# Four graph layers in one kernel: small steps at the seam between layer 0 and layer 1 put in another order

## The chip, the cores and the metric

The kernel runs on one core of a Trainium2 chip. The metric is the device time of one execution in microseconds; less is better. A core has five engines with a queue each, which run side by side and wait for one another by semaphores: TensorE (PE in the profile; its weight loads are PEld), VectorE (DVE), ScalarE (ACT), GpSimd (POOL) and SyncE (SP), which here only issues DMAs. ScalarE issues DMAs too. An engine works off its queue in order: an instruction that waits holds everything behind it.

## What is computed

`x` is 2708 x 128 and `adj` 2708 x 2708, f32, about 0.6% of it not zero. Four layers each add a graph network's answer to `x`; the change touches the end of layer 0 and the beginning of layer 1.

```python
# layer 0
h = relu(layernorm(x))
x = x + (adj.T @ h) / adj.sum(axis=0)[:, None]        # 1/deg, 0 where it is infinite
# layer 1
h = relu(layernorm(x))
s = h @ msg_w[:, :D].T                                # sources, by row i
d = h @ msg_w[:, D:].T                                # destinations, by column j
messages   = gelu(s[:, None, :] + d[None, :, :] + msg_b)
aggregated = einsum('ijd,ij->id', messages, adj)
u = gelu(concat([h, aggregated]) @ upd_w.T + upd_b) + h
x = x + layernorm(u) * ln_w + ln_b
# layer 2: GRU cell on relu((adj @ h) @ W_msg.T + b_msg); layer 3: two attention heads, masked by adj
```

## The kernel before

Rows are cut into 22 tiles of 128 (the last has 20 rows), and these into six groups of four (`GROUPS`, the last of two). All order is written out by hand; there is no scheduler that moves instructions.

**Layer 0** goes over sets (c, s): 512 columns `c` by the 512 rows of group `s`. For c = 0 to 4 the loop at L733 takes each set in turn. `load_cut` (L314) brings it in on SP, five sets ahead. `list_cut` (L344) lets DVE find, per row and block of 128 columns, the eight largest values (`val`, L356) and their places (`col`, L358). `work_cut` (L366) has TensorE transpose the set block by block into PSUM (`p_T`, L403, three banks), ScalarE copy each transposed strip to `aT` with its sum (the degrees, L410) and send it to memory as `adjT` (L364), and TensorE multiply the set with `h` (L388). The narrow last columns (c = 5, 148 wide, tiles `z`) are loaded early, and their sets are worked in pieces (`PARTS`) behind sets (4,1) to (4,4).

`work_cut` takes a second argument, a generator of small steps; after each `aT` copy it runs one of them. `next_steps(c, s)` (L516) gives these for c > 0: copy the finished sums of the group before (`lift`), scale and add them to `x` (`spread`, which needs `inv_deg` from `invert` on DVE), then sums and squares over the rows (`sum_rows`, `sum_squares`, the latter ending in a chain of GpSimd steps on `flat`), then the normalized rows of layer 1 (`normal_rows`). A group of layer 1's rows is turned (`turn_rows`), multiplied into destinations (`destinations`, bf16 lead `d`), and the rest split off in two further bf16 parts (`take_lead` L247 on DVE, `split_rest` L253 on ScalarE and L254 on GpSimd).

**Layer 1** works on the listed edges only. For each row tile t one needs:

- `count_some` or `count_rows`: how many entries each row has in each block (`rows_n`), on DVE; `rank` (L551): a matmul that sums these counts over the rows before, giving `ends`; `spread_ends` (L558): a copy of `ends` four times over
- `select_rows` (L601): a 128 x 2816 comparison that makes `sel`, the row of every edge slot; its shifted copy `later` goes by DMA (L620, L621); `finish_rows` (L625) subtracts it
- the values in three bf16 parts in `xb`, of which there are two, by the parity of t: `lead_of` (ScalarE, L568), `less_lead` (DVE, L586, into a tile named `hot`), `pass_rest` (ScalarE L590, GpSimd L591, and `describe_columns`, GpSimd L580 and L581)
- `fetch` (L639): 22 small matmuls `y<-xb,sel` that move values and columns to edge slots; `place` (L652 to L673, DVE) picks `value` and `where` from them
- `pass_on` and `spread_columns`: `where` is transposed, copied (`where_T`, L691), written to memory (`passed`, L693) and read back to all partitions (`spread`, L699); `columns` (L973, DVE) compares it to `cols`
- `put_values` (L956, eight GpSimd steps) and `put_more` (L965, ScalarE): the value of each edge placed on its row.

Then `period(t, opening)` (L1127) runs row tile t's main work in six pieces k: `combine` (L1012 with `sel` and the sources `s`, L1016 with `cols` and the destinations `d`) into `p_m` (two banks), GELU on ScalarE (`g`, L1024), `gather` (L1037), with the preparation of tiles t+1 to t+4 in between. Period 0 differs: its opening steps stand in a table (`opening`, L1231), run at the head of each k, and what periods before it would have prepared is made during layer 0 and in the `run(...)` list ahead of the periods (L1226).

So the last sets of layer 0 carry steps of layer 1: `count_some` and `list_last` in (4,0) to (4,2), `rank(0, 3)` of three tiles in (4,1), `select_rows(0)` after it, `finish_rows(0)` after (4,2), `pass_rest(0)` and `fetch(0)` after (4,3), `place(0)` after (4,4), `last_destinations` within (4,5), and a list of small steps at the end of layer 0 (L813 to L826).

PSUM banks of the pool `ps` are two and go round: `p_r`, the two `y` of tile 0, `p_h`, `p_d`, `p_w` and `p_s` take turns, each waiting until the one before last has been read.

Of the kernel before, what the change touches and what calls it, by code (L numbers as in the profile page):

```python
# [30 lines left out]
P = 128  # L31
# [14 lines left out]
S = 8  # L46
# [14 lines left out]
def listed_layers(ctx: ExitStack, tc: tile.TileContext, x, adj, w, out, flag):  # L61
# [8 lines left out]
    def bank(name):  # L70
        return ps.tile([P, CH], F32, tag="ps", name=name)
# [194 lines left out]
    def sum_squares(g):  # L266
        t, k = GROUPS[g]
        for q in range(t, t + k):
            junk = pool.tile([P, D], F32, name="junk")
            nc.scalar.activation(  # L270
                junk, xs[:, q, :], AF.Square, bias=flat[:, 0, q : q + 1], accum_out=flat[:, 1, q : q + 1]
            )
            if q == t + k - 1:
                shift, ve, rstd, tmp = (flat[:, r, t : t + k] for r in range(4))
                nc.gpsimd.tensor_scalar(ve, ve, 1.0 / D, EPS, ALU.mult, ALU.add)
                nc.gpsimd.tensor_tensor(rstd, ve, minus_half[:, 0:k], ALU.pow)
                nc.gpsimd.tensor_tensor(tmp, rstd, rstd, ALU.mult)
                nc.gpsimd.tensor_tensor(tmp, tmp, ve, ALU.mult)
                nc.gpsimd.tensor_scalar(tmp, tmp, -0.5, 1.5, ALU.mult, ALU.add)
                nc.gpsimd.tensor_tensor(rstd, rstd, tmp, ALU.mult)  # L280
                nc.gpsimd.tensor_tensor(shift, shift, rstd, ALU.mult)
            yield

    def normal_rows(dst, g, rstd=None, shift=None):
        t, k = GROUPS[g]
        for q in range(k):
            r, b = (flat[:, 2, t : t + k], flat[:, 0, t : t + k]) if rstd is None else (rstd, shift)
            scale_rows([dst[:, t + q, 0:D]], [xs[:, t + q, :]], r[:, q : q + 1], b[:, q : q + 1], AF.Relu)
            yield
# [226 lines left out]
    def next_steps(c, s):  # L516

        off = 1 if c < LAST - 1 else 0
        stage = s - 1 - off
        if stage == -1:  # L520
            return lift(c - 1)
        if stage == 0:
            return spread(c - 1)
        if stage == 1:
            return sum_rows(c - 1)
        if stage == 2:
            return sum_squares(c - 1)
        if stage == 3:
            return normal_rows(h, c - 1)
        return last_destinations() if stage == 4 and c == LAST - 1 else ()  # L530

    def last_destinations():
        destinations(LAST - 2)
        yield
        pass_on(0)
        project(0)
        turn_sums(LAST)
        yield

    def list_last(n):  # L540
# [41 lines left out]

    def less_lead(t):
        dst, src = values_of(t)
        rest = state["x", t] = opener.tile([P, NB, S], F32, name="hot")
        nc.vector.tensor_tensor(rest, src, dst[0], ALU.subtract)  # L586

    def pass_rest(t):
# [93 lines left out]
    def pass_on(t):  # L682

        st = state[t]
        if t == 0:
            p = ps.tile([P, 2 * CH], BF16, tag="ps", name="p_w")
        else:
            p = rpool.tile([P, 2 * CH], BF16, tag="r", name="p_w")
        nc.tensor.transpose(p[:, 0:E], st.pop("where"), ident_h)
        turned_w = own_tile(t, [NB, E], BF16, "where_T")  # L690
        nc.scalar.copy(turned_w, p[0:NB, 0:E])  # L691
        st["passed"] = wdram.tile([NB, E], BF16, name="passed")
        nc.sync.dma_start(st["passed"], turned_w)  # L693
# [39 lines left out]
    for i, (c, s) in enumerate(order):  # L733
        g0, gk = GROUPS[s]
        list_cut(c, s, g0)
        if i == 0:
            state["f", 0] = factors(*state.pop(("m", -1)))
            list_cut(c, s, g0 + 1)
            state["m", 1] = moments(tiles_of(xs, *GROUPS[1]), "n4")
            list_cut(c, s, g0 + 2)  # L740
            state["f", 1] = factors(*state.pop(("m", 1)))
            list_cut(c, s, g0 + 3)
        else:
            for n in range(g0 + 1, g0 + gk):
                if c > 0 and s == (2 if c < LAST - 1 else 1) and n == g0 + 1:
                    invert(c - 1)
                list_cut(c, s, n)
            if c == LAST - 1:
                for n in {0: range(FIRST), 1: range(FIRST, 4), 2: range(4, HELD), LAST: range(NT - 2, NT)}.get(s, ()):
                    list_last(n)  # L750
                if s == 0:
                    count_some(0, FIRST)
                if s == 1:
                    count_some(FIRST, 1)
        if i + 1 < len(order):
            mask_near(*order[i + 1])
        if i > BEHIND and i - 1 - BEHIND + RING < len(order):
            load_cut(*order[i - 1 - BEHIND + RING])
        for z in {(LAST - 2, 3): (0,), (LAST - 2, 4): (1,), (LAST - 2, 5): (2,), (LAST - 1, 0): (3,), (LAST - 1, 2): (4,), (LAST - 1, 3): (5,)}.get(
            (c, s), ()  # L760
        ):
            load_cut(LAST, z)
        if (c, s) == (LAST - 1, 2):
            shift_rows(0)
        if c > 0 and s == (2 if c < LAST - 1 else 1):
            turn_sums(c - 1)
        if (c, s) == (LAST - 1, LAST):
            turn_rows(LAST - 2)
        work_cut(c, s, first_steps(s) if c == 0 else next_steps(c, s))
        if c > 1 and s == 3:  # L770
            split_rest(c - 2)
        if (c, s) == (LAST - 1, 3):
            pass_rest(0)
        if c > 1 and s == 0:
            turn_rows(c - 2)
        if c > 1 and s == 1:
            destinations(c - 2)
        if c > 1 and s == 2:
            take_lead(c - 2)
        if c == LAST - 1:  # L780
            if s == 1:
                ranked = rank(0, FIRST, bank("p_r"))
            for z in PARTS.get(s, ()):
                mask_near(LAST, z)
                work_cut(LAST, z)
            if s == 1:
                nc.vector.tensor_copy(*ranked)
                spread_ends(0)
                select_rows(0)
                lead_of(*values_of(0))  # L790
            if s == 2:
                less_lead(0)
                finish_rows(0)
            if s == 3:
                for q in range(2):
                    fetch(0, q)
            if s == LAST - 1:
                place(0)
                lead_of(*values_of(2))
                less_lead(2)  # L800
                for _ in lift(LAST):
                    pass

        if (c, s) == (1, 2):
            nc.sync.dma_start(msg_wT, w["msg_wT"])
        if (c, s) == (2, 3):
            nc.sync.dma_start(msg_b, w["msg_b"].partition_broadcast(P))
            nc.gpsimd.tensor_copy(src_self[:, 0, :], msg_wT[:, 0, :])
            nc.gpsimd.tensor_tensor(src_self[:, 1, :], msg_wT[:, 0, :], msg_wT[:, 1, :], ALU.add)

    write_one()

    pass_rest(2)  # L813
    lead_of(*values_of(1))
    take_lead(LAST - 2, pool.tile([P, 4, D], F32, bufs=1, name="part_x"))
    add(LAST)
    measure(LAST)
    less_lead(1)
    add_bias(0, d_rest.rearrange("p (t c) d -> p t c d", t=2))
    spread_ends(1)  # L820
    split_rest(LAST - 2)
    for _ in lift(LAST - 1):
        pass
    turn_sums(LAST - 1)
    rows(LAST)
    pass_rest(1)  # L826
    ending.close()
    l0.close()

# [31 lines left out]
    with (  # L861
# [265 lines left out]
        def period(t, opening):  # L1127
# [6 lines left out]
            for k in range(GB):  # L1134
# [3 lines left out]
                if k == 0 and c and begun:  # L1138
                    pass_on(t + 1)
                    spread_columns(t + 1)  # L1140
                if k == 1 and a:
                    nc.vector.tensor_copy(*rank(t + 3, 1, rpool.tile([P, CH], F32, tag="r", name="p_r")))
                    spread_ends(t + 3)
                if k == 1 and last:
# [23 lines left out]
                if k == 2:  # L1168
                    if now and t % 2 == 0 and t + 2 < NT:
                        sources(t // 2 + 1)  # L1170
                    if a and begun:
                        select_rows(t + 3)
                        describe_rest(t + 3)
                    if now and t % 2 == 0 and t + 2 < NT:
                        sources_rest(t // 2 + 1)
                    if now and t + 4 < NT - 2:
                        count_rows(t + 4)
                if k == 1 and t == NT - 2:
                    check_lists()
# [43 lines left out]
        def take_pair(g):  # L1223
# [6 lines left out]
        )  # L1230
        opening = {  # L1231
            1: ((turn_rows, 4), (fetch_both, 1), (select_rows, 2), (put_more, 0, 1)),
            2: ((destinations, 4), (put_more, 0, 2), (put_more, 0, 3), (place, 1), (take_lead, 4), (finish_rows, 2)),
            3: ((split_rest, 4), (pass_on, 1), (spread_columns, 1), (put_more, 0, 4), (put_more, 0, 5)),
            4: ((fetch_both, 2), (find_rows, 1), (put_values, 1)),
            5: ((place, 2),),
        }
# [880 lines left out]
```

## Time and profile before

| | us |
|---|---|
| median of 3 runs | 987.94 (986.31 to 989.44) |
| the profiled execution | 986.58 |
| its span on the core | 984.8 |
| TensorE busy, granted clock | 911.1 (93%), 0.968 |
| VectorE busy | 797.0 (81%) |
| ScalarE busy | 531.8 (54%) |
| GpSimd busy | 444.1 (45%) |

The page of the profile gives the busy time of each engine, a picture of the span in 40 slices, and the costliest groups of instructions. The answers on the trace give the same by stretch of time, and timelines: start, busy time, engine, line and operation, and in brackets how long the engine stood idle before it and what released it. A releaser is inferred: where a matmul that had long been done is named, it was another, often a DMA. By the timeline, layer 0's last product on TensorE (L388) ends at 195.87 us, period 0 begins in earnest at 205.76, and period 1 at 230.53. The stretches around these, with the busy time of each engine, the granted clock of TensorE and the DMA engines' share:

| stretch, us | PE | DVE | ACT | POOL | PE clock | DMA |
|---|---|---|---|---|---|---|
| 170 to 175 | 3.81 | 5.00 | 5.00 | 1.20 | 1.00 | 0.70 |
| 175 to 180 | 1.40 | 5.00 | 1.00 | 4.59 | 0.82 | 0.24 |
| 195 to 200 | 2.23 | 4.79 | 2.07 | 2.50 | 0.87 | 0.41 |
| 200 to 205 | 1.93 | 4.61 | 3.51 | 2.27 | 0.50 | 0.59 |
| 215 to 220 | 3.72 | 2.98 | 1.61 | 1.35 | 1.00 | 0.05 |
| 220 to 225 | 0.79 | 4.95 | 4.41 | 4.66 | 0.76 | 0.14 |
| 225 to 230 | 5.00 | 4.05 | 2.48 | 5.00 | 0.56 | 1.01 |

### The profile page before, as it was taken

The numbers are of one execution on the slowest core, as the hardware profiler recorded it, in microseconds if no ns is written. First come the engines' busy times: TensorE is split into PE (matmuls) and PEld (weight loads), VectorE is DVE, ScalarE is ACT, GpSimd is POOL, SyncE is SP. The second block draws the span as 40 slices with busy tenths as digits, with TensorE's granted clock in tenths as the row PEclk, the third lists the DMA queues.
The fourth block names the chain that finished last, engine by engine and source line by source line (L and its number), as shares of the span: only waits on it lengthen the run. The fifth ranks groups of instructions, "written<-read, shape, count | busy, mean of one in ns | idle before, by whom it ended". The sixth has DMA issues, their size and how long they took to land. (4 is left out here: it accounts for less than half of the span.)

```text
span 984.8 us, 21973 instructions
## 1 busy us (share of the span) xinstructions
PE 911.1 (93%) x7948; PEld 742.5 (75%) x7948; DVE 797.0 (81%) x2753; ACT 531.8 (54%) x1561; POOL 444.1 (45%) x524
## 2 busy tenths in 40 slices
PE   6799999768999999899999999999789999999983
PEld 3465556558999999898999444444678999999972
DVE  7999999788988989889674756566689877997793
ACT  5766776656666756676566123433222553655242
POOL 5402221369976787969765634444111300430132
PEclk9999999978999999999999899999899999999996
DMA  9899998325543434323215355564301674456000
GB/s 334 286 354 365 359 368 296 125 94 160 169 129 117 149 115 135 120 81 132 91 62 190 119 190 208 194 237 134 93 6 57 211 245 151 145 186 208 1 17 15
DMA packets 81736, 163.61 MB, mean 166 GB/s; under 512 B 9100, under 2 KB 27056, under 8 KB 81618
## 3 DMA queue, kind: packets, MB, share of 16 engines
q1 hardware_dynamic: 62518, 129.98, 40.8%
q10 hardware_dynamic: 19100, 32.13, 9.0%
q8 instruction: 64, 1.05, 0.5%
q14 instruction: 54, 0.44, 0.1%
HBM read 115.47 MB, written 30.87 MB: 149 GB/s over the span
## 5 line engine op out<-in xcount | busy, mean ns | idle before, releaser
L1327 PE MATMUL att<-hv,wt 128*128 128x129 f32 x1672 | 195.7, 278 | 7.9 <-DVE wt L1297 6.4
L956 POOL TENSOR_SCALAR put<-count,line,value 128x128 f32<-128x128 f32 x176 | 197.6, 1134 | 11.1 <-DVE value L673 10.4
L1327 PEld LDWEIGHTS att<-hv,wt 128*128 128x128 f32 x1672 | 191.9, 194 | 10.9 <-DVE wt L1297 8.9
L1016 PE MATMUL p_m<-d,cols 128*128 128x128 bf16 (+1 forms) x1452 | 162.6, 221 | 9.2 <-DVE cols L973 4.3
L1012 PE MATMUL p_m<-s,sel 128*128 128x128 bf16 x1452 | 162.4, 221 | 5.0 <-ACT g L1024 4.9
L1297 DVE SCALAR_TENSOR_TENSOR wt<-row,lift,mask 128x1024 f32<-128x1024 f32 (+1 forms) x132 | 138.8, 1083 | 22.2 <-PE att L1327 22.2
L121 POOL TENSOR_TENSOR n_r<-n_r,minus_half 128x4 f32<-128x4 f32 (+1 forms) x28 | 38.9, 1389 | 237.7 <-DVE n_r L120 236.0
L1037 PE MATMUL agg<-put,g 128*128 128x128 f32 (+1 forms) x968 | 126.8, 284 | 0.0
L1037 PEld LDWEIGHTS agg<-put,g 128*128 128x128 f32 x968 | 116.2, 196 | 2.4 <-issue 0.2
L388 PE MATMUL sums<-a,h 128*128 128x512 f32 x220 | 113.9, 613 | 1.6 <-ACT h L137 1.6
L1488 PE MATMUL p_agg<-a,hs 128*128 128x512 f32 (+2 forms) x264 | 108.8, 554 | 2.8 <-DMA a<-adjT 2.8
L1012 PEld LDWEIGHTS <-sel 128*128 128x128 bf16 x1452 | 103.9, 99 | 9.0 <-issue 8.3
L1016 PEld LDWEIGHTS <-cols 128*128 128x128 bf16 (+1 forms) x1452 | 101.9, 99 | 10.1 <-DVE cols L973 5.0
L1024 ACT ACTIVATE g<-p_m 128x512 f32<-128x512 f32 x132 | 72.7, 552 | 63.8 <-PE agg L1037 45.0
L403 PEld LDWEIGHTS p_T<-ident,a 128*128 128x128 f32 (+1 forms) x440 | 55.4, 144 | 60.7 <-issue 43.1
L965 ACT ACTIVATE put<-mine,value 128x128 f32<-128x128 bf16 x308 | 100.6, 392 | 0.0
L358 DVE FIND_INDEX8 col<-val,a 128x8 uint16<-128x128 f32 x327 | 91.6, 298 | 0.0
L410 ACT ACTIVATE aT<-p_T 128x512 f32<-128x512 f32 (+2 forms) x132 | 71.1, 541 | 27.5 <-PE p_T L403 26.6
L1488 PEld LDWEIGHTS p_agg<-a,hs 128*128 128x128 f32 (+1 forms) x264 | 47.5, 193 | 50.6 <-issue 46.3
L403 PE MATMUL p_T<-ident,a 128*128 128x128 f32 (+1 forms) x440 | 70.5, 281 | 11.9 <-DMA a<-in_adj 6.2
L1450 ACT ACTIVATE hs<-hs 128x1354 f32<-128x1354 f32 (+1 forms) x44 | 58.5, 1330 | 39.9 <-DMA hs<-in_adj 39.5
L356 DVE MAX8 val<-a 128x8 f32<-128x128 f32 x327 | 79.4, 289 | 0.0
(297 smaller groups left out, 1529.0 us busy)
## 6 DMA issues: line engine op xcount, KB each, us to landing
hs<-in_adj SPq DMA_DIRECT2D x42, 677.0 KB
adjT<-aT ACTq DMA_DIRECT2D x50, 512.0 KB
a<-adjT SPq DMA_DIRECT2D x20, 1280.0 KB
a<-in_adj SPq DMA_DIRECT2D x24, 1024.0 KB
spread<-passed SPq DMA_DIRECT2D x22, 704.0 KB
later<-sel SPq DMA_DIRECT2D x22, 616.0 KB
cols_a<-in_adj SPq DMA_DIRECT2D x11, 320.0 KB
row<-own_d ACTq DMA_DIRECT2D x10, 256.0 KB
```

What stands on the lines that cost most here:

```text
L356: nc.vector.max(val[0:m, n, b, :], v)
L358: nc.vector.max_index(col[0:m, n, b, :], val[0:m, n, b, :], v)
L388: nc.tensor.matmul(accs[c][:, 0:w], h0[0:m, n, :], a[0:m, n - g0, t0 * P - lo : t0 * P - lo + w], start=(n == 0), stop=(n == NT - 1),)
L403: nc.tensor.transpose(p[0:k, i * iw + q * P : i * iw + q * P + m], a[0:m, q, e : e + k], ident[0:m, 0:m])
L956: nc.gpsimd.tensor_scalar(st["put", 0][:, b, :], count, st["line"][:, b : b + 1], st["value"][:, b : b + 1], ALU.is_equal, ALU.mult,)
L965: nc.scalar.activation(st["put", 1][:, b - HP, :], st["mine"][:, b - HP, :], AF.Identity, scale=st["value"][:, b : b + 1])
L1012: nc.tensor.matmul(p[:, b - b0, :], st["sel"][:, b, :], s3[:, q, t % 2, :], start=(q == 0), stop=False)
L1016: nc.tensor.matmul(p[:, b - b0, :], st["cols"][0:kb, b, :], d3[0:kb, b, q, :], start=False, stop=(q == 2))
L1037: nc.tensor.matmul(agg, g[:, b - 4 * k, :], put, start=(b == 0), stop=False)
L1297: nc.vector.scalar_tensor_tensor(wt[:, 0:n], row[:, k, c : c + n], lift[:, j, k : k + 1], mask[:, j, c : c + n], op0=ALU.max, op1=ALU.mult,)
L1327: nc.tensor.matmul(banks[s // 3][:, s % 3, :], wt[:, q * P : (q + 1) * P], hv[:, j, k, :], start=(v < 2 and s // 3 not in touched), stop=( ...
L1488: nc.tensor.matmul(pa[:, 0:n], h[0:k, j, :], a[0:k, j - j0, 0:n], start=(j == 0), stop=(j == NT - 1))
```

## The change

No arithmetic is changed. The steps that move:

- Ranks of four row tiles at once: `list_last(3)` and `count_some(3)` move from set (4,1) to (4,0), `rank` covers tiles 0 to 3, tile 4 is counted in set (4,2), and period 0 loses its rank matmul and its `count_rows(4)`.
- `pass_rest(0)` becomes the first small step within set (4,3); before it came behind the whole set.
- `project(0)` and the leads of tiles 2 and 1 become the first small step within set (4,4).
- `turn_rows(3)` moves between the two z parts behind (4,4), and `destinations(3)` and `pass_on(0)` ahead of set (4,5).
- `less_lead(1)` (now into a tile named `picked`), `spread_ends(1)` and `add_bias(0)` follow `place(0)` and `less_lead(2)`; `pass_rest(2)`, `pass_rest(1)` and `turn_sums(5)` become the first small step within set (4,5).
- In period 0's opening, `split_rest(4)` and `finish_rows(2)` change places: the first goes to the head of k=2, the second to that of k=3.

```diff
         if stage == 2:
-            return sum_squares(c - 1)
+            squares = sum_squares(c - 1)
+            return in_turn(in_order((pass_rest, 0)), squares) if c == LAST - 1 else squares
         if stage == 3:
-            return normal_rows(h, c - 1)
-        return last_destinations() if stage == 4 and c == LAST - 1 else ()
-
-    def last_destinations():
-        destinations(LAST - 2)
-        yield
-        pass_on(0)
-        project(0)
-        turn_sums(LAST)
+            last = c == LAST - 1
+            return in_turn(in_order((project, 0), (lead_of, *values_of(2)), (lead_of, *values_of(1))), normal_rows(h, c - 1)) if last else normal_rows(h, c - 1)
+        if stage == 4 and c == LAST - 1:
+            return in_order((pass_rest, 2), (pass_rest, 1), (turn_sums, LAST))
+        return ()
+
+    def in_order(*steps):
+
+        for step, *numbers in steps:
+            step(*numbers)
         yield
...
     def less_lead(t):
         dst, src = values_of(t)
-        rest = state["x", t] = opener.tile([P, NB, S], F32, name="hot")
+        if t == 1:
+            rest = opener.tile([P, NB, 4, S], F32, name="picked").rearrange("p b q s -> p (b q s)")[:, 0 : NB * S]
+            rest = rest.rearrange("p (b s) -> p b s", s=S)
+        else:
+            rest = opener.tile([P, NB, S], F32, name="hot")
+        state["x", t] = rest
         nc.vector.tensor_tensor(rest, src, dst[0], ALU.subtract)
...
-                for n in {0: range(FIRST), 1: range(FIRST, 4), 2: range(4, HELD), LAST: range(NT - 2, NT)}.get(s, ()):
+                for n in {0: range(FIRST + 1), 2: range(4, HELD), LAST: range(NT - 2, NT)}.get(s, ()):
                     list_last(n)
                 if s == 0:
                     count_some(0, FIRST)
-                if s == 1:
                     count_some(FIRST, 1)
+                if s == 2:
+                    count_some(FIRST + 1, 1)
...
         if (c, s) == (LAST - 1, LAST):
-            turn_rows(LAST - 2)
+            destinations(LAST - 2)
+            pass_on(0)
         work_cut(c, s, first_steps(s) if c == 0 else next_steps(c, s))
         if c > 1 and s == 3:
             split_rest(c - 2)
-        if (c, s) == (LAST - 1, 3):
-            pass_rest(0)
...
-                ranked = rank(0, FIRST, bank("p_r"))
+                ranked = rank(0, FIRST + 1, bank("p_r"))
             for z in PARTS.get(s, ()):
                 mask_near(LAST, z)
                 work_cut(LAST, z)
+                if z == LAST - 1:
+                    turn_rows(LAST - 2)
...
                 place(0)
-                lead_of(*values_of(2))
                 less_lead(2)
+                less_lead(1)
+                spread_ends(1)
+                add_bias(0, d_rest.rearrange("p (t c) d -> p t c d", t=2))
...
-    pass_rest(2)
-    lead_of(*values_of(1))
     take_lead(LAST - 2, pool.tile([P, 4, D], F32, bufs=1, name="part_x"))
     add(LAST)
     measure(LAST)
-    less_lead(1)
-    add_bias(0, d_rest.rearrange("p (t c) d -> p t c d", t=2))
-    spread_ends(1)
     split_rest(LAST - 2)
...
     rows(LAST)
-    pass_rest(1)
...
-                if k == 1 and a:
+                if k == 1 and a and not begun:
+                    spread_ends(t + 3)
+                elif k == 1 and a:
                     nc.vector.tensor_copy(*rank(t + 3, 1, rpool.tile([P, CH], F32, tag="r", name="p_r")))
                     spread_ends(t + 3)
...
-                    if now and t + 4 < NT - 2:
+                    if now and begun and t + 4 < NT - 2:
                         count_rows(t + 4)
...
-            2: ((destinations, 4), (put_more, 0, 2), (put_more, 0, 3), (place, 1), (take_lead, 4), (finish_rows, 2)),
-            3: ((split_rest, 4), (pass_on, 1), (spread_columns, 1), (put_more, 0, 4), (put_more, 0, 5)),
+            2: ((destinations, 4), (put_more, 0, 2), (put_more, 0, 3), (place, 1), (take_lead, 4), (split_rest, 4)),
+            3: ((finish_rows, 2), (pass_on, 1), (spread_columns, 1), (put_more, 0, 4), (put_more, 0, 5)),
```

## The prediction

> **What bounds the kernel now.** I read the page's slices first, to find the stage in which the change lives.
>
> ```profile
> PE   6799999768999999899999999999789999999983
> DVE  7999999788988989889674756566689877997793
> PEclk9999999978999999999999899999899999999996
> ```
>
> A slice is 24.6 us. TensorE is at 9 nearly everywhere; the weak stretch is slices 7 to 9 (172 to 246 us): the end of layer 0 and period 0 of layer 1, where every edit lies. From 230 us to 300 us TensorE is busy without a gap (busy time by stretch), so an earlier start of period 1 is kept. TensorE's own timeline for 172 to 226 us shows the holes:
>
> ```profile
> 178.60 0.86 PE L639 MATMUL y<-xb,sel 128*128 128x37 bf16 x22 [4.76 <-POOL xb L581]
> ...
> 199.06 0.70 PE L150 MATMUL p_h<-ident,hs 128*128 128x128 f32 x2 [1.85 <-ACT hs L137]
> ...
> 205.76 0.50 PE L1016 MATMUL p_m<-d,cols 128*128 128x128 bf16 x3 [3.51 <-DVE cols L973]
> ...
> 218.31 0.72 PE L639 MATMUL y<-xb,sel 128*128 128x37 bf16 x22 [0.54 <-DVE sel L625]
> ...
> 221.86 0.22 PE L1016 MATMUL p_m<-d,cols 128*128 128x128 bf16 x1 [2.60 <-ACT d L253]
> 224.42 0.27 PE L1016 MATMUL p_m<-d,cols 128*128 128x128 bf16 x1 [2.35 <-POOL d L254]
> ```
>
> The bracket is TensorE's idle time and its releaser. The timeline of all engines tells what delayed the first releaser:
>
> ```profile
> 170.24 0.34 DVE L586 TENSOR_TENSOR hot<-val,xb 128x176 f32<-128x176 f32 x1
> 173.72 0.19 POOL L275 TENSOR_SCALAR flat<-flat 128x4 f32<-128x4 f32 x1 [8.85 <-ACT junk L270]
> 174.03 0.37 ACT L590 CAST xb<-hot 128x176 bf16<-128x176 f32 x1
> 176.39 1.15 POOL L254 TENSOR_TENSOR d<-d_r,d 128x512 bf16<-128x512 f32 x1
> 177.50 0.54 POOL L591 TENSOR_TENSOR xb<-hot,xb 128x176 bf16<-128x176 f32 x1
> ```
>
> `hot` is ready at 170.58; ScalarE copies it at 174.03 behind a set of sums, and GpSimd takes it at 177.50 behind the `flat` chain and `d`. In period 0:
>
> ```profile
> 216.62 1.62 DVE L625 TENSOR_TENSOR sel<-sel,later 128x2816 bf16<-128x2816 bf16 x1 [1.46 <-DMA later<-sel]
> 218.88 0.40 ACT L568 CAST s<-sb 128x256 bf16<-128x256 f32 x1 [2.83 <-DVE sb L728]
> 221.20 0.60 ACT L253 CAST d<-d_r 128x512 bf16<-128x512 f32 x1
> 221.88 2.49 POOL L254 TENSOR_TENSOR d<-d_r,d 128x512 bf16<-128x512 f32 x1
> 227.68 1.05 DVE L973 TENSOR_SCALAR cols<-spread,part 128x2816 bf16<-128x2816 bf16 x1 [0.53 <-DMA spread<-passed]
> ```
>
> `d_r` is ready at 215.17, but the copy at 221.20 stands behind `s`, and `s` behind a DVE that waits for a DMA.
>
> **The change, part by part.** Times are those of this one execution: 986.58 us, span 984.8, 1.8 outside it. The median 987.94 lies 1.36 above it.
>
> *Ranks of four tiles.* The listing of row tile 3 (0.69 us, the step between two such listings at 147.37 and 148.05) and its count (0.24 + 0.34) move ahead of `invert(3)` on DVE, which has no gap from 120 to 182.9 us. So `inv_deg` comes 1.25 us later. ScalarE's `part_x` already waits 2.29 us for it, and TensorE's rank matmul at 155.38 already waits 0.36 us for `part_x`. That wait grows: **+1.25 us** on TensorE, busy after it up to 170.4. It could be nothing: at 165.9 to 169.7 ScalarE waits 1.50 and 1.73 us before two `aT` copies whose matmuls had long been done, so for `adjT` writes, and there the delay may drown. I take all of it. The count of row 4 moves from period 0 to this stretch: DVE +0.6 us up to `less_lead(0)` and `place(0)`. The rank matmul, its copy (0.17) and `rows_n` leave period 0, off the path.
>
> *`pass_rest(0)` one stage earlier.* Its four instructions (one ScalarE copy, three on GpSimd: 0.54, 0.36, 0.28) now follow the first `aT` copy of set (4,3). New wait: ScalarE stands for `hot` until 170.58 + 0.6 = 171.2, with the other `aT` copies and four sums queued behind it, and TensorE behind those (three transpose banks). Second `aT` copy 170.66 -> 171.5, so about 0.9 us, which runs beside the 1.25 above. GpSimd is idle until 173.72: `xb` is done at 171.6 + 1.2 = 172.8 and `sel` at 172.7. TensorE comes at 173.84 + 1.25 = 175.1. The 4.76 us go, 1.25 come: `y` starts at 175.1 instead of 178.60, **-3.5**.
>
> [...] Here the three GpSimd steps fall on the `sel` subtraction (L625, two inputs). The row for it: `d` L254 takes 1.15 us alone and 2.49 beside a two-input DVE step, itself 2.09 for 1.62. At 2.2 times, 1.2 us become 2.6, and `xb` is done at 174.2: still 0.9 before TensorE. [...] I take nothing.
>
> *Set (4,4), the two z parts, set (4,5).* Both leads now come after the first `aT` of (4,4) (+0.3 us on ScalarE, which is ahead there), `project(0)` moves here with 1.08 us of matmuls. TensorE at full clock: `y` 0.72, four steps of 1.30, 1.08: 175.1 -> 182.1 (before 185.67). z4 takes 1.9 (185.67 to 187.55 in the timeline) -> 184.0. Then the transposes of `h` need a `ps` bank, held until `place(0)` has read it. DVE's listing ends at 182.9 + 0.6, the first `picked` at 184.8: new wait 0.8 us, replacing none. After it z5 1.6 (187.55 to 189.14), `destinations(3)` 1.0, `p_w` 0.2, from 185.4 -> 188.2; `turn_sums(5)` now stands before the second pair of transposes and waits for `take_lead` (189.3); pair 0.7, products 2.07: layer 0 ends on TensorE at about 192.4 instead of 195.87, **-3.5**. The SP queue's order is the same in both built programs, so no DMA issue overtakes another; `passed` only goes out sooner.
>
> *Between the layers.* DVE works nearly without a break from 192.6 to 205.7, and TensorE's 3.51 us wait for `cols` is its queue. `less_lead(1)` 0.34, `add_bias` 0.68, `spread_ends` 0.20 leave it for the DVE gap before 190.1 (4.56 us). But they stood in the gap left by GpSimd's power (195.77 to 196.49), so mostly nothing is won: power now waits behind the two `pass_rest` (to 192.1) and ends at 192.8 instead of 196.5. From there the chain is the same: -3.7; ScalarE also loses the 0.35 `xb` copy between `hs` and `s`. I take `cols` at 201.7: **-4.0** so far.
>
> *Period 0* (in old times, all shifted by 4.0). `split_rest(4)` comes before `sources`: ScalarE copies `d` at 215.6 to 216.1, GpSimd, free at 216.35, has `d` by 217.6 (218.9 if stretched); TensorE needs it at 219.1 or later. Both holes, 2.60 + 2.35, go. `finish_rows(2)` now stands behind `sb` and `s_r`, which wait for ScalarE: `d`, `g` (0.58), `s` (0.40) end at 217.1, `s_r` at 217.5, so `sel` at 219.1 instead of 218.24. TensorE, free at 217.8, waits 1.3 instead of 0.54. Then k=4 1.33, k=5 held for `g` until 221.7, gathers 2.0 (the row at 215.77): 224.4. Next late is `cols(1)`: `where_T` 219.3 instead of 221.71, and the two DMA hops took 227.68 - 221.71 = 6.0 us: 225.3, +1.0 for the compare: period 1 at 226.2 instead of 230.53: **-4.3**.
>
> [...] The rows are less kind: in 220 to 225 the granted clock is 0.76 and in 225 to 230 it is 0.56, after gaps of 2.60 and 2.35. If half clock comes at 217.8, k=4, k=5 and gathers take 3.4 us more (227.8), and `cols(1)` no longer matters: -2.7. [...]
>
> Sum: 3.5 + 0.5 + 4.3 = 8.3 us off 984.8, so 978.3 for such an execution; on the median 979.6. I forecast **980.0**. From 230 us on nothing changes.
>
> **The rivals.** *Half the gain* (chance 0.22): layer 0 gains but period 0 is cold or `cols(1)` lands later, or the ScalarE stand at `hot` costs a further microsecond: 4 to 5 us, 983.5. For: DMA-bound 166 to 170. Against: idle GpSimd. *Hidden anyway* (0.08): another chain carries the end of layer 0, e.g. DVE's listing to 182.9, which the change lengthens by 0.6; then `place(0)` sets the pace and both gains shrink to within 3 us: 986.5. Against: DVE stood 4.56 us after `place(0)`. *Slower* (0.08): ScalarE at `hot`. It now blocks the `aT` stream for DVE's `less_lead(0)`; each microsecond that DVE is later than 171.2 passes, after 1.3 us of bank slack, into TensorE and the `adjT` writes. It decides if `hot` comes after about 180; with 4 us more from a cold period 0 that is +4: 992. DVE's unbroken stream speaks against it.
>
> **How the numbers follow.** Forecast 0.62 (977.5 to 982.5), half 0.22, hidden 0.08, slower 0.08. The low end is no cost for the ranks (-1.25) and cheaper waits, 976.5; the high end takes in the half gain and its bounds, 985.5. About 0.3%, 3 us, is what a measurement here can tell from no change: faster 0.62 + 0.20 = 0.82, same 0.10, slower 0.08.
>
> **What would show it.** The 4.76 at `y` gone and the rank matmul's 0.36 at about 1.6; `cols(0)` at about 201.7 with a gap still near 3.5; the 2.60 and 2.35 gone, a gap of 1 to 2 at `y` of tile 2, one at `cols(1)`; period 1 at about 222. I am wrong if ScalarE's wait for `hot` exceeds 2 us or if TensorE after 222 shows new gaps.

## The result and the profile after

The changed kernel takes 983.61 us (median of 20 runs, 977.37 to 987.14) where the kernel before, on the same chip, took 987.83 (20 runs, 982.57 to 990.32). The ratio is 0.9952, with an interval of 0.9939 to 0.9965: 4.2 us less, half of the 8.3 that the steps added up to. The profiled execution took 985.46 us, its span 983.6, at a granted clock of 0.966.

The page of the changed kernel has the same three rows again, a digit for each slice of 24.6 us.

```profile
PE   6799999978999999899999999999789999999983
DVE  7999999897988989889674656566689977997793
PEclk9999999779999999999999899999899999999996
```

TensorE went from 7, 6 and 8 to 9, 7 and 8 in slices 7 to 9 (172 to 246 us): the holes there are partly filled. The clock, though, is now at 7 in slice 7 as well, where it was at 9, and the same matmuls are busy for longer at half clock (three of `p_m<-d,cols` take 0.53 us at 205.32, with 0.50 granted from 205 to 206 us, and 0.33 at 207.81, with 0.97 from 207 to 210), so part of this 9 is slowness and no work won.

TensorE's timeline of the changed kernel, with the instructions that answer to those shown of before:

```profile
174.77 0.71 PE L646 MATMUL y<-xb,sel 128*128 128x37 bf16 x22
184.92 0.66 PE L150 MATMUL p_h<-ident,hs 128*128 128x128 f32 x4 [1.46 <-DVE picked L670]
...
203.43 0.50 PE L1021 MATMUL p_m<-d,cols 128*128 128x128 bf16 x3 [2.86 <-DVE cols L978]
...
216.98 0.72 PE L646 MATMUL y<-xb,sel 128*128 128x37 bf16 x22 [1.45 <-DVE sel L632]
...
223.82 0.34 PE L1021 MATMUL p_m<-d,cols 128*128 128x128 bf16 x3 [1.43 <-DVE cols L978]
...
231.12 0.51 PE L646 MATMUL y<-xb,sel 128*128 128x37 bf16 x11 [2.88 <-POOL xb L583]
```

The 4.76 us before the first `y` are gone, and so are the 2.60 and 2.35 in period 0. The waits at `p_h`, at `y` of tile 2 and at `cols(1)` are the new ones that the prediction named. Period 1 starts at 223.82 instead of 230.53. The last line is the one that it did not name: in period 1, `y` of tile 3 waits 2.88 us for GpSimd. Before, there was no wait at that place.

A landmark makes the loss countable: the two matmuls that close a row tile (`agg<-ident,gs`). The table gives their times for tiles 0 and 1, and period 1 between them. The changed kernel was profiled a second time, beside the last experiments (983 us median of 20 runs, ratio 0.9961, 0.9945 to 0.9977).

| profiled execution | close of tile 0, us | close of tile 1 | period 1 |
|---|---|---|---|
| before | 234.71 | 248.29 | 13.58 |
| after | 227.84 | 245.85 | 18.01 |
| after, second profile | 226.28 | 244.31 | 18.03 |

The rows of before, and then of the second profile, from the close of tile 0 to that of tile 1:

```profile
234.71 0.39 PE L1045 MATMUL agg<-ident,gs 128*128 128x128 f32 x2
234.94 0.43 PE L639 MATMUL y<-xb,sel 128*128 128x37 bf16 x11
248.29 0.39 PE L1045 MATMUL agg<-ident,gs 128*128 128x128 f32 x2
```

```profile
226.28 0.39 PE L1050 MATMUL agg<-ident,gs 128*128 128x128 f32 x2
229.77 0.51 PE L646 MATMUL y<-xb,sel 128*128 128x37 bf16 x11 [3.10 <-POOL xb L583]
244.31 0.39 PE L1050 MATMUL agg<-ident,gs 128*128 128x128 f32 x2
```

So 8.43 us are won at the close of tile 0 in the second profile (6.87 in the first), and 4.45 of them are lost within the next 18 us. What remains, 3.98, is about what the runs show (4.2, and 3.9 by the ratio of the second time). From there to the close of tile 7 every period has the length that it had before, to 0.01 us.

GpSimd's timeline of the kernel before, around the values of tile 3 (L573, L580 and L581 fill `xb`):

```profile
224.36 8.84 POOL L956 TENSOR_SCALAR put<-count,line,value 128x128 f32<-128x128 f32 x8
233.17 0.53 POOL L573 TENSOR_TENSOR xb<-v_r,xb 128x176 bf16<-128x176 f32 x1
233.65 0.35 POOL L580 CAST xb<-col 128x176 bf16<-128x176 uint16 x1
233.94 0.27 POOL L581 COPY xb<-ends 128x22 bf16<-128x22 bf16 x1
```

The same four in the second profile of the changed kernel:

```profile
215.88 11.56 POOL L961 TENSOR_SCALAR put<-count,line,value 128x128 f32<-128x128 f32 x8
227.41 1.80 POOL L575 TENSOR_TENSOR xb<-v_r,xb 128x176 bf16<-128x176 f32 x1
229.16 0.35 POOL L582 CAST xb<-col 128x176 bf16<-128x176 uint16 x1
229.44 0.27 POOL L583 COPY xb<-ends 128x22 bf16<-128x22 bf16 x1
```

The first column is the start, the second the time that all of the row's steps took. The eight steps of `put_values(1)` start 8.48 us sooner, so GpSimd's queue did move along with the rest. But they now take 11.56 us instead of 8.84, and the first step of `xb` 1.80 instead of 0.53: `xb` is complete at 229.71 instead of 234.21, only 4.50 sooner. TensorE comes 8.43 sooner, and before the change it had 0.73 us of slack (234.94, its `y`, less 234.21). 8.43 - 4.50 - 0.73 = 3.20, and the wait measured there is 3.10. Most of the other 1.35 of the 4.45 is TensorE's clock, at 0.75 between 230 and 235 us after this wait, where it was 1.00: from this `y` to the next (232.57) TensorE takes 2.80 us, and before the change it took 1.61 (234.94 to 236.55).

What lies beside the stretched steps can be read on DVE. In the second profile of the changed kernel, DVE's rows beside these steps begin with

```profile
215.29 1.55 DVE L608 TENSOR_TENSOR mine<-count_h,lead 128x1792 bf16<-128x1792 bf16 x1
216.77 1.61 DVE L608 TENSOR_TENSOR sel<-count_h,ends 128x2816 bf16<-128x2816 bf16 x1
...
227.22 1.60 DVE L608 TENSOR_TENSOR sel<-count_h,ends 128x2816 bf16<-128x2816 bf16 x1
```

and the first step of `xb`, at 227.41, lies on the third of them. Before the change, the `sel` of tile 3 had run at 221.27 to 223.36, under `d` on GpSimd (the 2.49 us shown with the prediction), and was over when the eight steps began. The stretch went from one GpSimd instruction to another. That steps on DVE with two inputs are its cause can be estimated from the rows. In e1 below, the last four steps of `put_values(0)`, from 209.24 us, have no wide two-input DVE step beside them and take 3.10 us, so eight would take 6.2; in the first profile of the changed kernel eight from 240.89 us, with none beside them either, take 6.22. Before the change two wide steps lie beside the eight (`mine` 1.08 and `sel` 1.62): 8.9, and 8.84 was measured. After it four do (0.96 us of `mine`, then 1.61, 1.07 and 1.63): 11.5, and 11.56 was measured. (For the eight of tile 0 in e1, with three beside them, the same count gives 10.6 where 9.95 was measured; in the first profile of the changed kernel it was 9.94, from 204.04 us.) By this estimate the eight steps lose about what the wide DVE steps last. The step at 227.41 ends at 229.21, and the third `sel` at 228.82: it too looks as if it had stood until that step was over. The count leaves out DVE steps with one input tile, but in e1 a step of `xb` takes 1.16 us, and in e10 1.17 (from 223.67), where `cols`, with one, runs first beside it (in e10 from 223.40, for 1.05). No run took these DVE steps away alone.

### The profile page after: what moved, and what is told of

It reads as the page before. It is cut to its first block, busy times and chain, and to the rows that moved or that the text cites. A ratio compares the mean times of both kernels' runs of the same rounds, so it can differ in the third digit from the quotient of the medians.

```text
span 983.6 us, 21968 instructions
## 1 busy us (share of the span) xinstructions
PE 913.6 (93%) x7947; PEld 743.5 (76%) x7947; DVE 797.6 (81%) x2752; ACT 531.3 (54%) x1561; POOL 442.5 (45%) x524
## 3 DMA queue, kind: packets, MB, share of 16 engines
q8 instruction: 64, 1.05, 0.5%
## 5 line engine op out<-in xcount | busy, mean ns | idle before, releaser
L1334 PEld LDWEIGHTS att<-hv,wt 128*128 128x128 f32 x1672 | 192.2, 194 | 10.6 <-DVE wt L1304 8.7
L358 DVE FIND_INDEX8 col<-val,a 128x8 uint16<-128x128 f32 x327 | 89.6, 286 | 0.0
```

The lines of the kernel that those rows point to most:

```text
L358: nc.vector.max_index(col[0:m, n, b, :], val[0:m, n, b, :], v)
L1334: nc.tensor.matmul(banks[s // 3][:, s % 3, :], wt[:, q * P : (q + 1) * P], hv[:, j, k, :], start=(v < 2 and s // 3 not in touched), stop=( ...
```

## The experiments

Two theories stood for the missing half. **A**: it is lost in period 1, behind GpSimd's eight steps. **B**: it is lost at the end of layer 0, where the first profile of the changed kernel shows half clock from 186 to 206 us (0.61 from 186 to 189, then 0.50) after the 1.46 us wait at `p_h`. Each ratio is to the kernel before, run beside it on the same chip.

**The eight steps cut in two** (e1): the changed kernel, with four of them behind the values of tile 3.

```diff
-        def put_values(t):
+        def put_values(t, first=0, end=HP):
...
-            for q, n in enumerate((HP, NB - HP)):
+            for q, n in enumerate((HP, NB - HP) if first == 0 else ()):
...
-            for b in range(HP):
+            for b in range(first, end):
...
-            4: ((fetch_both, 2), (find_rows, 1), (put_values, 1)),
-            5: ((place, 2),),
+            4: ((fetch_both, 2), (find_rows, 1), (put_values, 1, 0, 4)),
+            5: ((put_values, 1, 4), (place, 2)),
```

> The changed kernel, with GpSimd's eight placement steps of tile 1 in period 0 cut in two: four before and four after the three steps that complete xb of tile 3. Theory A (what is missing of the forecast was lost in period 1, where the small matmuls y of tile 3 wait 2.88 us for xb behind these eight steps, and the cold clock after it): the wait goes, the time from close of tile 0 to close of tile 1 falls from 18.0 to 13.6 to 14.5 us, and the time falls by 3 to 4.4 us against the changed kernel, to 979 to 980.5. Theory B (it was lost at the end of layer 0, where TensorE runs at half clock from 186 to 206 us after its 1.46 us wait for the bank): within 1 us of the changed kernel, 983 to 984.5, because another wait takes the place of this one.

Measured: 974.68 us (972.89 to 976.83, 5 runs), ratio 0.9883 (0.9861 to 0.9906). On GpSimd the values of tile 3 now follow four steps, and on TensorE no wait is left at `y` of tile 3:

```profile
215.81 5.57 POOL L961 TENSOR_SCALAR put<-count,line,value 128x128 f32<-128x128 f32 x4
221.34 1.16 POOL L575 TENSOR_TENSOR xb<-v_r,xb 128x176 bf16<-128x176 f32 x1
...
223.60 0.27 POOL L583 COPY xb<-ends 128x22 bf16<-128x22 bf16 x1
```

`xb` is complete at 223.9, and the matmul takes it at 226.43. Tile 1 closes at 239.78, 8.51 us sooner than before the change, and period 1 takes 13.58. A holds. The ratio gives 11.5 us (9.2 to 13.7); 8.5 of them lie ahead of the close of tile 1. The rest, some 3 us (0.7 to 5.2 by the interval), has no place in the trace that would repeat, and stays open: periods 12 and 16 vary from one profiled execution to the next (17.1 to 20.1 and 16.0 to 18.4), whatever the kernel.

**The exchange in period 0 alone** (e2): the kernel before, with only this.

```diff
-            2: ((destinations, 4), (put_more, 0, 2), (put_more, 0, 3), (place, 1), (take_lead, 4), (finish_rows, 2)),
-            3: ((split_rest, 4), (pass_on, 1), (spread_columns, 1), (put_more, 0, 4), (put_more, 0, 5)),
+            2: ((destinations, 4), (put_more, 0, 2), (put_more, 0, 3), (place, 1), (take_lead, 4), (split_rest, 4)),
+            3: ((finish_rows, 2), (pass_on, 1), (spread_columns, 1), (put_more, 0, 4), (put_more, 0, 5)),
```

> The kernel before, with one edit of the change alone: in period 0's opening split_rest(4) and finish_rows(2) change places. Theory A: the two holes of 2.60 and 2.35 us go and period 1 begins some 4 us sooner, but the wait for xb of tile 3 on GpSimd appears in period 1 and takes most of it back: 986 to 988, a gain of 0 to 2 us. Theory B: the 4 us stay, 983.5 to 984.5.

Measured: 984.87 us (14 runs), ratio 0.9987 (0.9971 to 1.0003). The holes of 2.60 and 2.35 are gone and tile 0 closes 2.9 us sooner, at 231.80, but period 1 takes 17.86: in this kernel, too, the eight steps take 11.23 us, and `y` of tile 3 waits:

```profile
234.96 0.51 PE L639 MATMUL y<-xb,sel 128*128 128x37 bf16 x11 [2.77 <-POOL xb L581]
```

Alone, the exchange is worth nothing that can be told from zero: what it wins goes into this wait and the lower clock after it (three matmuls of `p_m` take 0.53 us up to 237.50 and 0.33 from 238.20 on).

**Another bank for `p_h`** (e3), so that the transposes of group 3 need not wait for `place(0)`; and **both** (e4: e3 with e1's cut).

```diff
-        turn(hT[:, c : c + n], bank("p_h1"), lambda q: h[:, t + q, :], k, t, nc.scalar.copy)
+        p = turnp.tile([P, CH], F32, name="p_T") if g == LAST - 2 else bank("p_h1")
+        turn(hT[:, c : c + n], p, lambda q: h[:, t + q, :], k, t, nc.scalar.copy)
```

> The changed kernel, with the transposes of row group 3 in a bank of the pool of the other transposes, so that they don't wait until place(0) has read y. Theory A: the 1.46 us wait goes and the clock may stay at 1.00 from 185 to 195 us, but what layer 1 gains from it (about 1 us, since DVE's queue sets when cols of tile 0 come) is lost again at y of tile 3: 982.5 to 984, no change that can be told. Theory B: 980 to 981.5, and the runs lie closer together.

> Both edits, the split placement steps and the other bank. Theory A: as the split alone or up to 1 us better, 978 to 980. Theory B: as the other bank alone, 980 to 981.5.

Measured: e3 981.35 us, ratio 0.9948 (0.993 to 0.9967), no different from the changed kernel's 0.9952. The wait at `p_h` is gone, the clock stays at 1.00 from 186 to 192 us, tile 0 closes at 225.48, and period 1 takes 19.59: all of it is lost there. e4 took 975.45 us, ratio 0.9889 (0.9868 to 0.991), as e1. B falls as the cause of the missing half.

**Layer 0's edits alone** (e6): the changed kernel with the two lines of the exchange put back as they were.

> The changed kernel with period 0's opening in the order it had before: the edits of layer 0 alone. Theory A (the gain of layer 0 is real, and the changed kernel loses it in period 1, where GpSimd's eight steps of put_values(1) stand ahead of the values of tile 3): here these eight steps move forward together with everything around them, so the matmul y of tile 3 waits as little as before the change (under 0.5 us), period 1 takes about 13.6 us, and the whole gain of layer 0 stays: 3.5 to 4.5 us, ratio 0.9955 to 0.9965. Rival B (layer 0's gain is lost again later whatever period 0 does): no more than 1 us, ratio above 0.999, with the loss in a period that the trace shows.

Measured: 983.5 us (15 runs), ratio 0.9964 (0.9947 to 0.998): 3.6 us, the size that A gave. The expectation of no wait missed: `y` of tile 3 waits 1.74 us, mostly since L583 takes 1.65 instead of 0.27 beside a `sel`, and period 1 takes 15.48. By the trace 5.2 us are won at the close of tile 0 and 1.9 lost in period 1.

**The cut alone** (e7, the kernel before with e1's diff) and **the exchange with the cut** (e9, e2 with e1's diff).

> The kernel before with nothing changed but put_values(1) cut in two, four GpSimd steps ahead of the values of tile 3 and four behind. Theory A: before the change TensorE came to tile 3 too late to wait for GpSimd, so the cut brings nothing: ratio 0.999 to 1.001, period 1 at 13.6 us as it was. Rival C (the cut is an improvement of its own, which would explain why e1 came out some 2 us better than the wait it took away): 2 to 3 us faster, ratio 0.997 to 0.998.

> The kernel before with period 0's two steps exchanged and put_values(1) cut in two: e2_opening_alone with the cut. Theory A: e2 closed tile 0 2.9 us sooner and lost all of it in period 1 (17.9 us instead of 13.6); with the cut period 1 takes about 13.6 us and the 2.9 stays, so 982.5 to 984 beside 986.5, ratio 0.996 to 0.998. Rival B (the exchange brings nothing in any case): ratio 0.999 to 1.001.

Measured: e7 987.41 us, ratio 1.0003 (0.9988 to 1.0018); e9 981.85 us (22 runs), ratio 0.9961 (0.9946 to 0.9976), with period 1 at 13.57. The cut is worth nothing where TensorE comes late, and it turns the exchange from nothing into 3.9 us. (The intervals of e2 and e9 just overlap; in the traces the cut brings period 1 from 17.86 back to 13.57.) As A says.

**The ranks of four undone in e1** (e8): three tiles are ranked and counted in layer 0 again, and the fourth in period 0, of which the diff shows the first part.

```diff
-                for n in {0: range(FIRST + 1), 2: range(4, HELD), LAST: range(NT - 2, NT)}.get(s, ()):
+                for n in {0: range(FIRST), 1: range(FIRST, 4), 2: range(4, HELD), LAST: range(NT - 2, NT)}.get(s, ()):
...
-                ranked = rank(0, FIRST + 1, bank("p_r"))
+                ranked = rank(0, FIRST, bank("p_r"))
```

> e1_puts_split with the ranks as before the change: three tiles ranked in layer 0, the fourth in period 0. The prediction's step says the ranks of four cost 1.25 us on TensorE at the rank matmul; by it this run is 1.2 us faster than e1 (973.5 beside 974.7), the rank matmul's wait about 0.4 us and the close of tile 0 at 225.0 instead of 226.2 in the trace. Theory A (the cost drowns, since the degrees and the copies of set (4,3) wait for something else anyway): the first y at the same time within 0.4 us and the whole within 0.7 us of e1. Theory D (the count, the rank matmul and its copy in period 0 cost DVE time on the way to cols(1)): this run is slower than e1 by up to 1 us, with the close of tile 0 later.

Measured: 976.5 us (972.98 to 980.84, 6 runs), ratio 0.9882 (0.9851 to 0.9913), beside e1's 0.9883; a difference of 1 us would be lost in this interval. The trace is finer: the rank matmul stands at 155.40 instead of 156.67 and the first `y` at 173.77 instead of 174.79, so the ranks do cost 1.3 us there, and 1.0 at `y`, as the prediction's step has it. Then both kernels wait for the same `picked` on DVE (184.26 and 184.83), where 0.6 of it is left. The close of tile 0, expected at 225.0, came at 229.07: in this profiled execution TensorE was at half clock from 185 us on (0.50 in each stretch from 186 to 207), which hides what the ranks cost at that place.

**`pass_rest(0)` alone** (e5): the kernel before with this one step moved.

```diff
-            return sum_squares(c - 1)
+            return in_turn(rest_first(), sum_squares(c - 1)) if c == LAST - 1 else sum_squares(c - 1)
...
+    def rest_first():
+        pass_rest(0)
+        yield
...
-        if (c, s) == (LAST - 1, 3):
-            pass_rest(0)
```

> The kernel before with one step moved: pass_rest(0) becomes the first small step within set (4,3). Theory A (the 4.76 us hole at y is the one wait that held the end of layer 0; the other moves there only follow it): the hole goes, y starts at about 174, layer 0's last product ends some 4 us sooner, cols(0) comes at about 202, and the run is 3 to 4 us faster, ratio 0.996 to 0.997, as with all of layer 0's edits together (0.9964). Rival E (the moves of the transposes, of project(0) and of the steps on DVE carry the gain; alone the hole's time is given back before cols(0)): cols(0) later than 204, no more than 1.5 us faster.

Measured: 983.67 us (18 runs), ratio 0.9958 (0.994 to 0.9976), as much as the whole change. TensorE's timeline:

```profile
173.75 0.71 PE L643 MATMUL y<-xb,sel 128*128 128x37 bf16 x22
184.24 0.66 PE L150 MATMUL p_h<-ident,hs 128*128 128x128 f32 x4 [0.72 <-DVE picked L667]
...
200.53 0.50 PE L1018 MATMUL p_m<-d,cols 128*128 128x128 bf16 x3 [3.50 <-DVE cols L975]
```

`cols(0)` comes at 200.53, 5.2 us sooner than before the change, and 1.3 sooner than with all of layer 0's edits (201.88 in e6). So the other moves in layer 0 win nothing at `cols(0)`; together with the ranks they lose 1.3 us there. The timelines divide it. About 0.7 is there at `p_h` (184.24 here, 184.92 in e6); with the ranks undone, e8 has 184.26, so these are the ranks. Another 0.9 comes between `p_h` and the sums at `p_s`: 7.09 us here, 7.98 in e6. Here both z parts are done ahead of `p_h`; with `turn_rows(3)` between them, the second, 1.6 us, stands behind the wait for `picked`, while `project(0)`, 0.9 us, went the other way. No run moved `turn_rows(3)` alone. Some 0.2 is won again up to `cols(0)`. Period 1 keeps its 13.58 here, and the 5.2 stay until the close of tile 7.

**`cols(0)` ahead of the rows of group 4** (e10: e1 with this), and **an attempt at more** (e11).

```diff
-            (spread_columns, 0), (select_rows, 1), (take_sources, 0), (turn_rows, 5), (sources_rest, 0), (add, 4), (measure, 4),
-            (destinations, 5), (take_pair, 5), (split_rest, 5), (columns, 0), (rows, 4), (put_values, 0), (finish_rows, 1),
+            (spread_columns, 0), (select_rows, 1), (take_sources, 0), (turn_rows, 5), (sources_rest, 0), (columns, 0), (add, 4), (measure, 4),
+            (destinations, 5), (take_pair, 5), (split_rest, 5), (rows, 4), (put_values, 0), (finish_rows, 1),
```

> e1_puts_split with the comparison cols(0) moved on DVE ahead of add(4) and measure(4). It tells what TensorE's 3.51 us wait for cols(0) is. Theory A (it is DVE's queue: spread had landed by 195): TensorE has cols(0) at about 198.3 instead of 201.8, but tile 0's first GELU stands on ScalarE behind the rows of group 4, which come 0.9 us later, and the transposes of group 4 stand on TensorE behind those: the wait returns there, at p_h, and the run is within 1 us of e1 (974 to 976). Rival F (the wait is for the DMA of spread): TensorE still starts on cols(0) after 201, with a wait above 3.

Measured: 982.08 us (11 runs), ratio 0.9947 (0.9929 to 0.9966): slower than e1 by 6 us, where up to 1 was expected. TensorE's timeline:

```profile
198.29 0.52 PE L1021 MATMUL p_m<-d,cols 128*128 128x128 bf16 x3
...
204.88 1.63 PE L150 MATMUL p_h<-ident,hs 128*128 128x128 f32 x4 [4.15 <-ACT hs L137]
```

Half of the expectation came true: the 3.51 us were DVE's queue, not the DMA, and they return as 4.15 at `p_h`. What was not expected is the price. The matmuls of k=0 are now done at half clock ahead of the wait (0.50 from 195 to 207 us), and the clock is still 0.53 from 207 to 210 us, where e1 has 1.00; tile 0 closes at 228.54 instead of 226.20. The other 4 us of the difference are not in this trace, and stay open.

e11 moves the rows of group 4, their transposes and tile 1's fetch further back, and two steps of `put_values(0)` forward.

```diff
-            (spread_columns, 0), (select_rows, 1), (take_sources, 0), (turn_rows, 5), (sources_rest, 0), (columns, 0), (add, 4), (measure, 4),
-            (destinations, 5), (take_pair, 5), (split_rest, 5), (rows, 4), (put_values, 0), (finish_rows, 1),
-            (spread_ends, 2), (find_rows, 0),
+            (spread_columns, 0), (select_rows, 1), (take_sources, 0), (turn_rows, 5), (sources_rest, 0), (columns, 0), (put_values, 0, 0, 2), (add, 4), (measure, 4),
+            (destinations, 5), (take_pair, 5), (split_rest, 5), (put_values, 0, 2), (finish_rows, 1),
+            (spread_ends, 2),
...
-            1: ((turn_rows, 4), (fetch_both, 1), (select_rows, 2), (put_more, 0, 1)),
-            2: ((destinations, 4), (put_more, 0, 2), (put_more, 0, 3), (place, 1), (take_lead, 4), (split_rest, 4)),
-            3: ((finish_rows, 2), (pass_on, 1), (spread_columns, 1), (put_more, 0, 4), (put_more, 0, 5)),
+            1: ((rows, 4), (find_rows, 0), (select_rows, 2), (put_more, 0, 1)),
+            2: ((fetch_both, 1), (put_more, 0, 2), (put_more, 0, 3), (place, 1)),
+            3: ((turn_rows, 4), (finish_rows, 2), (destinations, 4), (take_lead, 4), (split_rest, 4), (pass_on, 1), (spread_columns, 1), (put_more, 0, 4), (put_more, 0, 5)),
```

> An attempt at a better version: e10_columns_first with the rows of group 4 moved into the head of k=1, their transposes and destinations into that of k=3, tile 1's fetch into that of k=2, and two of the eight GpSimd steps of put_values(0) ahead of measure(4). If the queues allow it, TensorE works from 198 on and meets its next limit at the first gathers, which need put_values(0), done at about 210 instead of 212.3: 1 to 2.5 us faster than e1, 972 to 974. If the later transposes leave d too late for k=4, or ScalarE's rows hold the GELUs, it is up to 2 us slower than e1, 977.

Measured: 983.05 us (22 runs), ratio 0.9961 (0.9948 to 0.9975). In this kernel tile 1's fetch stands behind ScalarE's copy that refills `xb` for tile 3, so it moves tile 3's leading values in place of its own: tile 1's are left out of the answer, and the time counts only as a sign. The fetch also waits for that copy (4.71 us), and the destinations then wait 3.18 for `hT`. By the time, the attempt gives back what e1 won.

**The changed kernel again.**

> The changed kernel itself once more, for a second profile and its time beside the others. Theory A: period 1 takes about 18 us again with a wait of 2 to 3 us at y of tile 3 behind GpSimd, ratio 0.994 to 0.9965. The half clock from 186 to 206 us was one execution's (it did not come in e1, e3, e4 and e6, it came in e8): it may or may not come again; where it doesn't, tile 0 closes at about 226.2 instead of 227.8.

Measured as in the table above. The half clock between 186 and 195 us did not come again, tile 0 closed at 226.28, and the loss in period 1 did: it belongs to the kernel, the half clock to one execution.

## Why the prediction was half right

The steps, by their own numbers, against the second profile of the changed kernel, whose clock is full from 161 to 192 us (1.00 in the stretches from 182 on, and four transposes take 0.60 us from 161.68 on; the kernel before was at 0.50 from 179 to 181, after the 4.76 us wait that is gone):

| step | forecast | measured |
|---|---|---|
| ranks: rank matmul | 156.6 | 156.70 |
| first `y` | 175.1 | 174.77 (first profile), 176.42 |
| new wait at `p_h` | 0.8 | 1.46 (first profile), none shown |
| end of layer 0 (sums at `p_s`) | 3.5 sooner | 196.55 to 192.87, 3.7 sooner |
| `cols(0)` | 201.7 | 201.86 |
| wait at `y` of tile 2 | 1.3 | 1.60 |
| start of period 1 | 222.2 | 222.26 |
| "From 230 us on nothing changes" | 0 | +4.45 |

- *Up to 222 us the sum is right.* It gave 8.3 us at the start of period 1, and the second profile has 230.53 - 222.26 = 8.27. In the first, a half clock at the end of layer 0 (0.50 from 189 us on) took 1.6 of them. One step between is off and did no harm: the second profile was at half clock from 157 to 161 us too (four transposes take 1.03 to 1.06 us instead of 0.60), after a wait of 1.87 us at the rank matmul, and its first `y` came at 176.42, 1.3 later than forecast. The slack at `p_h` took this in.
- *"From 230 us on nothing changes"* is the step that failed: `y` of tile 3 waited 3.10 us for GpSimd, and 4.45 were lost. It took TensorE's gapless stretch from 230 to 300 us for proof that the gain is kept. That stretch shows only that nothing was late by the old timetable; `xb` of tile 3 had 0.73 us of slack. It would have been seen by asking of GpSimd what was asked of TensorE: how far its queue moves along, and beside which DVE steps it then falls.
- *GpSimd's steps beside DVE's* were weighed at the wrong place. At `pass_rest(0)` "I take nothing" was right: L598 took 1.45 us instead of 0.54 beside the `sel` subtraction, and `xb` was complete at 173.72, a microsecond ahead of TensorE. In period 1 the same stretch, 2.72 and 1.27 us, decided.
- *Set (4,4) and the parts after it*: e5 shows that the moves behind `pass_rest(0)` won nothing at `cols(0)`. The end of layer 0 hangs on `picked`, on DVE: the first `y` at 174.77 or 176.42 gives the same `p_h` at 184.92 and 184.95 (in the second profile TensorE comes just as `picked` is there). The prediction let `turn_rows(3)` wait there and put the second z part, 1.6 us, behind it, without asking what that costs.
- *Clock.* In period 0 the waits of 1.45 to 1.60 kept full clock from 210 to 225 us in both profiles (1.00 in each stretch), and the sum had taken 4.3 us for period 0, not the 2.7 of a half clock. That gaps of 1.3 to 1.8 us would do so was the author's assumption, which no row of the kernel before showed: there the clock had fallen to 0.50 by 199 us, in a wait of 1.85 us that followed one of 0.68.
- *The rivals.* "Half the gain" named the time, 983.5, and none of its three reasons: period 0 stayed warm after 210, `cols(1)` waited 1.43 where 1.8 was forecast, and ScalarE stood 0.60 us for `hot`. That 983.61 lies within the range given, up to 985.5, is due to this rival's place in the range and not to the steps; so far it is luck. The sign set for being wrong, new gaps on TensorE after 222 us, is what came.

## What to carry to other kernels

Here a gain on the bounding engine was kept only as far as the producers of the following stretch came earlier too: take the slack of each of its inputs (here 0.73 us) from the trace before counting on it. GpSimd's queue, moved along in time, also came to lie beside other DVE steps, and the same eight steps took 11.56 us there instead of 8.84. And try the moves one at a time: one of them alone gave what all gave together, and a cut at the new wait gave 7 us more (e1, the fastest kernel here, with e4 and e8 beside it). Whether that one step with the exchange and the cut would do as well was not tried.

## What the runs showed of the hardware

The granted clock after a short wait was not the same from one profiled execution to the next: 0.50 after 1.46 us in one, 1.00 after 1.45 in another. The rows give busy time of each engine, then the clock and the DMA share, for the stretches 186 to 189 and 189 to 192 us; first the changed kernel, after a wait of 1.46 us at `p_h`, then e1, after 1.35.

```profile
186.00:189.00 3.00, 3.00 (x14) 2.53 (x14) 2.36 (x11) 1.50 (x10) 0.00 (x0) 0.61 0.14 39
189.00:192.00 3.00, 3.00 (x13) 1.73 (x12) 1.78 (x7) 1.89 (x8) 0.46 (x1) 0.50 0.05 11
```

```profile
186.00:189.00 3.00, 2.94 (x19) 2.23 (x19) 2.55 (x12) 2.27 (x13) 0.00 (x0) 1.00 0.14 39
189.00:192.00 3.00, 3.00 (x10) 1.19 (x10) 2.67 (x12) 2.30 (x11) 1.95 (x6) 1.00 0.31 79
```

e6 (1.43), e10 (1.45) and e11 (1.36) stayed at 1.00 there, e8 (1.79) fell to 0.50. The rank matmul shows the same: after a wait of 1.76 us e1 kept its pace (four transposes take 0.60 us at 157.49), after 1.87 the second profile of the changed kernel fell to half clock for some 3.5 us (1.06 at 157.62). In the first profile the half clock of 186 us was still there at 196, although TensorE, by the profile, which models the ends of matmuls, had been busy without a break. (From 195.5 to 205 us e1 is at 0.50 as well, after waits of 0.68 and 1.95.) The way back took 3.6 busy microseconds in e1 (201.79 to 205.4) and 4.9 in e10 (204.88 to 209.8). In the first profile and in e8 (185 to 196 us) more than 9 busy microseconds did not bring it back. So waits of 1.46, 1.79 and 1.87 us came before a fall to half clock, waits of 1.35 to 1.45 and of 1.76 did not, and no run told apart what decides between them.
